# Graph layer on one core: filter banks stored with both channel chunks in a row, taps and stores over two queues each, and two transposes issued earlier in every round

## The chip, the cores and the metric

One core of a Trainium2 chip. The metric is the device time in microseconds (us) of one execution of the whole program; lower is better. "TensorE" is called PE in the profile, the vector engine DVE, the scalar engine ACT, GpSimd POOL and SyncE SP. All results were correct against the reference.

## The reference, cut to what matters

```python
h = relu(layernorm(x))                       # x: (64 graphs, 256 nodes, 256 channels), fp32
xc = transpose(h, (0, 2, 1))
c = relu(bn1(conv1d(xc, conv1_w)))           # 1 x 1
c = bn2(conv1d(c, conv2_w, pad=8))           # 17 taps, 256 -> 256 channels
x_conv = transpose(relu(c + xc), (0, 2, 1))
s = h @ w_se.T + b_se                        # 3 columns
A = exp(-dist(s)) * adj                      # 256 x 256 per graph
x_nmp = A @ relu(h @ w_msg.T + b_msg)
gi = concat(x_conv, x_nmp) @ w_ih.T + b_ih   # gates of a GRU cell
gh = h @ w_hh.T + b_hh
out = x + gru(gi, gh, h)
```

## The kernel before

The 64 graphs are done in eight rounds of four pairs. The 17-tap convolution is done with a transform of length 16, so its weights are needed as **filter banks**, one per frequency bin. They are made once, in the start: a tile of taps is multiplied with a matrix of points, copied from PSUM to a staging tile `fo` by ACT, and stored to DRAM in `filt`. Every round loads the banks from there as `wb`.

```python
KG = P // TAPS                                # 7 channels x 17 taps = 119 partitions
NG = P // KG
REST = P - NG * KG
taps = stage.tile([KG * TAPS, DC * NG + 1, D], FP, name="taps")
# ...
for dc in range(DC):
    for h in range(3):
        load_taps(dc, h * NG // 3, (h + 1) * NG // 3, nc.sync)
# ...
filt = [dram.tile([DC, P, t.shape[1] // KG, D], FP, name=f"filt{n}") for n, t in enumerate(points)]

def filters(m, j):
    # ... two groups of taps of one channel chunk
    p = acc()                                 # 5 PSUM buffers, shared with conv1 and the gates
    for n, g in enumerate(groups):
        mm(p[:size * kinds, n * D:(n + 1) * D], points[m][:size * TAPS, :size * kinds],
           taps[:size * TAPS, g, :], D, start=True, stop=True)
    t = stage.tile([P, 2, D], FP, name="fo", bufs=6)
    nc.scalar.copy(...)
    nc.sync.dma_start(out=filt[m][dc, ...], in_=t[:size * kinds])
```

In what follows the **embedding** is `s`, the **message** `relu(h @ w_msg.T + b_msg)`, the **aggregation** its product with `A`, and the **gates** are the products with `w_ih` and `w_hh`. To **evict** is to copy a result from PSUM to a tile in SBUF. Each pair is normalised by DVE, transposed by PE, evicted with the relu by ACT to `hT`, and goes through `conv1`, also on PE:

```python
def transpose_h(i):
    HT[i] = work.tile([P, DC, W], FP, name="hT", bufs=6)
    for dc in range(DC):
        p = aux()                             # 3 PSUM buffers
        for j in range(G * MC):
            transpose(chunk(p, j // MC, j % MC), X[i][:, j, dc * P:(dc + 1) * P])
        nc.scalar.activation(HT[i][:, dc, :], p, AF.Relu)
    if i + 2 < B // G:
        load_x(i + 2, nc.scalar if i < 2 else nc.sync)

# the middle of a round
gates(i, 1)
aggregate(i + 2)
pace.flush(normed)
transpose_h(nxt + 1)
pace.flush(halved)
conv1(nxt + 1)
# ...
gates(i + 1, 0)
message(i + 3)
embed(i + 3)
pace.flush(normed)
transpose_h(nxt + 2)
conv1(nxt + 2)
```

In these traces ACT and PE take up their work in the order of the program, so where `conv1` follows its transposes at once, PE has nothing to do until ACT has evicted them.

Of the kernel before, what the change touches and what calls it, by code (L numbers as in the profile page):

```python
# [13 lines left out]
FP = mybir.dt.float32  # L14
# [283 lines left out]
def kernel(  # L298
# [26 lines left out]
    nc = tc.nc  # L325
    P = 128
    B, N, D = x.shape
    G = 2
    GB = 8
    PB = GB // G  # L330
    NB = B // GB
    DC = D // P
    MC = N // P
    W = G * N
    TAPS = c2_wT.shape[1]
# [9 lines left out]
    work = ctx.enter_context(tc.tile_pool(name="work", bufs=1))  # L345
    stage_ctx = ExitStack()
    stage = stage_ctx.enter_context(tc.tile_pool(name="stage", bufs=1))
# [55 lines left out]
    def mm(p, w, v, columns, **kw):  # L403
        nc.tensor.matmul(p, w, v, **kw)  # L404
        pace.tensor(columns)
# [75 lines left out]


    KG = P // TAPS
    NG = P // KG
    REST = P - NG * KG
    taps = stage.tile([KG * TAPS, DC * NG + 1, D], FP, name="taps")

    def load_taps(dc, a, b, eng):
        eng.dma_start(out=taps[:, dc * NG + a:dc * NG + b, :],  # L489
                      in_=c2_wT[dc * P + a * KG:dc * P + b * KG].rearrange("(g k) t o -> (k t) g o", k=KG))  # L490

    PASSES = [range(0, 6), range(6, 12), range(12, 16)]
# [1 line left out]
    for n, bins in enumerate(PASSES):  # L494
        f = filter_points(bins, TAPS)
        m = np.zeros((KG, TAPS, KG, f.shape[1]), np.float32)
        for k in range(KG):
            m[k, :, k] = f
        t = stage.tile([KG * TAPS, KG * f.shape[1]], FP, name=f"points{n}")
        nc.scalar.dma_start(out=t, in_=nc.inline_tensor(m.reshape(KG * TAPS, -1), name=f"points{n}").ap())  # L500
        points.append(t)
    for dc in range(DC):
        for h in range(3):
            load_taps(dc, h * NG // 3, (h + 1) * NG // 3, nc.sync)
        nc.sync.dma_start(out=taps[dc * REST * TAPS:(dc + 1) * REST * TAPS, DC * NG, :],  # L505
                          in_=c2_wT[dc * P + NG * KG:(dc + 1) * P].rearrange("k t o -> (k t) o"))

    ld = const.tile([P, W], FP, name="ld")
    rd = const.tile([P, W], FP, name="rd")
# [56 lines left out]



    filt = [dram.tile([DC, P, t.shape[1] // KG, D], FP, name=f"filt{n}") for n, t in enumerate(points)]

    def filters(m, j):

        kinds = filt[m].shape[2]
        groups = range(2 * j, min(2 * j + 2, DC * NG + 1))
        size = REST * DC if groups[0] == DC * NG else KG
        p = acc()
        for n, g in enumerate(groups):
            mm(p[:size * kinds, n * D:(n + 1) * D], points[m][:size * TAPS, :size * kinds],
               taps[:size * TAPS, g, :], D, start=True, stop=True)
        t = stage.tile([P, 2, D], FP, name="fo", bufs=6)  # L580
        nc.scalar.copy(t[:size * kinds, :len(groups)].rearrange("p n o -> p (n o)"),
                       p[:size * kinds, :len(groups) * D])
        if size == KG:
            dc, g = divmod(groups[0], NG)
            nc.sync.dma_start(out=filt[m][dc, g * KG:(g + 2) * KG].rearrange("(g k) t o -> (k t) g o", k=KG),
                              in_=t[:size * kinds])
        else:
            for dc in range(DC):
                nc.sync.dma_start(out=filt[m][dc, NG * KG:].rearrange("k t o -> (k t) o"),
                                  in_=t[dc * REST * kinds:(dc + 1) * REST * kinds, 0, :])  # L590


    WB = {}
# [1 line left out]
    def load_bin(b, n):  # L595
        b, n = b + n // BINS, n % BINS
        if b < NB:
            WB[b, n] = work.tile([P, DC, 3, D], FP, name="wb", bufs=3)
            kinds, m = 3 if n < BINS - 1 else 2, n // len(PASSES[0])
            first = 3 * (n - PASSES[m][0])  # L600
            nc.sync.dma_start(out=WB[b, n][:, :, :kinds, :].rearrange("p k t o -> p k (t o)"),
                              in_=filt[m][:, :, first:first + kinds, :].rearrange("k p t o -> p k (t o)"))


    def operands(n):
# [11 lines left out]

    def products(b, m):
        load_bin(b, 2 * m + 2)
        p = [acc() for _ in range(3)]  # L620
        for n in range(2):
            for kind, v in enumerate(operands(2 * m + n)):
                if v is None:
                    continue
                for o in range(DC):
                    for k in range(DC):
                        mm(p[kind][:, (n * DC + o) * P:(n * DC + o + 1) * P],
                           WB[b, 2 * m + n][:, k, kind, o * P:(o + 1) * P],
                           v[:, k::DC, 0, :], P, start=(k == 0), stop=(k == DC - 1))
        load_bin(b, 2 * m + 3)  # L630
        p1 = work.tile([P, W], FP, name="p1")
        pv = [t.rearrange("p (n a e) -> p a n e", n=2, e=NW) for t in (p1, p[1], p[2])]
        if m < 7:
            nc.scalar.copy(p1, p[0])
            if m < 4:
                re, im = Yv(m % 2, m // 2 * 2, 2), Yv(m % 2, 4 + m // 2 * 2, 2)
            elif m < 6:
                re, im = Yu(m - 4, 0, 2), Yu(m - 4, 2, 2)
            else:
                t = Yu.t[:, :, :, 6:8, :].rearrange("p a c n e -> p n a c e")  # L640
                re, im = t[:, 0], t[:, 1]
            pace.vector(2 * W, pace.pe + PSUM)
            nc.vector.tensor_sub(re, pv[0], pv[2])
            nc.vector.tensor_add(im, pv[0], pv[1])
        else:
            half = W // 2
            nc.scalar.copy(p1[:, :half], p[0][:, :half])
            nc.scalar.mul(Yu(0, 4)[:, :, 0, :], p[0][:, half:].rearrange("p (a e) -> p a e", e=NW), 0.5)
            nc.scalar.mul(Yu(1, 4)[:, :, 0, :], p[1][:, half:].rearrange("p (a e) -> p a e", e=NW), 0.5)
            pace.vector(W, pace.pe + PSUM)  # L650
            nc.vector.tensor_sub(Yu(0, 5)[:, :, 0], pv[0][:, :, 0], pv[2][:, :, 0])
            nc.vector.tensor_add(Yu(1, 5)[:, :, 0], pv[0][:, :, 0], pv[1][:, :, 0])
# [143 lines left out]

    w_ih = const.tile([P, 2 * DC, 3 * D], FP)
    w_hh = const.tile([P, DC, 3 * D], FP)
    chunks = (range(NG // 2), range(NG // 2, NG + 1))
    steps = [(m, j) for m, dc in ((0, 0), (1, 0), (0, 1), (2, 0), (1, 1), (2, 1)) for j in chunks[dc]]  # L800
    transpose_h(0)
    norm(1)
    w_se = const.tile([P, DC, KD], FP)
# [22 lines left out]
    forward()  # L826
    for j, (m, n) in enumerate(steps[PB * 4:]):
        filters(m, n)
        if j == 20:
            load_bin(0, 0)  # L830
            load_bin(0, 1)
    nc.scalar.dma_start(out=w_hh, in_=hh_wT.rearrange("(k p) o -> p k o", p=P))
# [15 lines left out]
    for b in range(NB):  # L848
# [50 lines left out]
        gates(i, 0, wait)  # L899
        transpose_a(i + 2)  # L900
        gates(i, 1)
        aggregate(i + 2)
        pace.flush(normed)
        transpose_h(nxt + 1)
        pace.flush(halved)
        conv1(nxt + 1)
        stats, scale = norm_steps(nxt + 2)
# [2 lines left out]
        pace.add(scale, normed)  # L910
        pace.flush(joined[1])
        gates(i + 1, 0)
        message(i + 3)
        embed(i + 3)
        pace.flush(normed)
        transpose_h(nxt + 2)
        conv1(nxt + 2)
        stats, scale = norm_steps(nxt + 3)
        pace.add(stats)
# [65 lines left out]
```

## Time and profile before

| | before |
|---|---|
| median of three runs | 1997.85 us (1995.75 to 2002.09) |
| PE busy | 1922 us, 96% of the span |
| idle of PE in the start, 0 to 220 us | 47 us |
| waits of PE in the seven steady rounds | 19.4 us, 14 waits, all for `hT` |
| last filter matmul | 111.7 us |

In the profile a group such as `PE L404 MATMUL acc<-hT,w_c` is read as: engine, source line, operation, the tile written and the tiles read; L404 is the line of the helper that issues every matmul. `[2.47 <-ACT hT L537]` at its end means that the engine was idle for 2.47 us before it and that ACT's write of `hT` ended this.

The dearer of the two places of a round is seen in the timeline of PE in the kernel before (start in us, duration in us, what):

```profile
731.73 1.04 PE L408 MATMUL aux<-ident,x 128*128 128x128 f32 x8
735.24 5.32 PE L404 MATMUL acc<-hT,w_c 128*128 128x512 f32 x8 [2.47 <-ACT hT L537]
...
971.67 3.70 PE L404 MATMUL acc<-hT,w_c 128*128 128x512 f32 x8 [2.47 <-ACT hT L537]
```

The last line is the same place one round later. The timeline of ACT shows what the eviction waits behind, the first and the last of the four small activations of `embed`:

```profile
731.93 0.68 ACT L668 ACTIVATE ld<-aux,b_se 3x512 f32<-3x512 f32 x1 [0.30 <-PE aux L404]
...
733.88 0.68 ACT L671 ACTIVATE rd<-aux,b_se 3x512 f32<-3x512 f32 x1
734.59 1.09 ACT L537 ACTIVATE hT<-aux 128x512 f32<-128x512 f32 x2
```

### The profile page before, as it was taken

The page shows a single profiled execution, that of the slowest core. Times are in us where ns is not written, and L with a number is a line of the kernel's source. Part 1 is how long each engine was busy: PE and PEld are TensorE (multiplying, and loading weights), DVE is VectorE, ACT ScalarE, POOL GpSimd, SP SyncE. Part 2 cuts the span into 40 slices and gives each one's busy share as a digit, 9 for nine tenths or more (in the row PEclk, how much of TensorE's full clock was granted, in tenths as well). Part 3 has the DMA queues.
Part 4 walks back from the last instruction along what each step waited for, and adds up shares of the span by engine and source line. Part 5 has one row for each costly group of instructions (what it writes and reads, how often), then busy time and mean ns, then how long its engine had stood idle before and what let it go on. Part 6 is the DMA issues. An engine that isn't in the chain of part 4 may idle for free.

```text
span 1999.7 us, 21268 instructions
## 1 busy us (share of the span) xinstructions
PE 1922.1 (96%) x7966; PEld 1210.7 (61%) x7966; DVE 1401.8 (70%) x2668; ACT 642.2 (32%) x1050; POOL 170.1 (9%) x250
## 2 busy tenths in 40 slices
PE   4879999999999999999999999999999999999997
PEld 2668445875459645695457854486445954568543
DVE  3668738995489945998369963899559993689522
ACT  1533322243222432235222433134322252233321
POOL 3000000010100000010000100001010100000000
PEclk8899999999999999999999999999999999999999
DMA  5785012640217212271115501263032711145010
GB/s 152 222 253 179 22 42 54 176 135 12 78 33 223 73 33 68 78 220 31 41 50 153 161 15 49 62 190 106 23 78 53 233 32 48 32 108 157 11 42 21
DMA packets 91699, 187.12 MB, mean 94 GB/s; under 512 B 20524, under 2 KB 37420, under 8 KB 91596
## 3 DMA queue, kind: packets, MB, share of 16 engines
q1 hardware_dynamic: 60722, 131.87, 21.1%
q0 software_dynamic: 27792, 50.07, 10.9%
q10 hardware_dynamic: 3082, 3.83, 0.7%
q8 instruction: 62, 1.02, 0.2%
q14 instruction: 41, 0.34, 0.0%
HBM read 156.55 MB, written 29.10 MB: 93 GB/s over the span
## 4 chain that ended last, share of the span: by engine, by line
PE 92%; DMA 4%; ACT 2%; SPq 1%; issue 1%; POOL 0%; ACTq 0%; DVE 0%; POOLq 0%; DVEq 0%
PE acc L404 72%; PE aux L404 16%; PE aux L408 3%; DMA wb<-filt 1%; DMA taps<-in_c_wT_dram 1%; DMA filt<-fo 1%; SPq L489 1%; ACT hT L537 0%; SPq L505 0%; DMA bn_m<-in_bn_m_dram 0%; ACT ld L670 0%; ACT rd L671 0%; ACT ld L668 0%; ACT xnm L720 0%; ACT rd L669 0%
## 5 line engine op out<-in xcount | busy, mean ns | idle before, releaser
L404 PE MATMUL acc<-hT,w_hh 128*128 128x512 f32 x768 | 350.6, 592 | 0.0
L404 PE MATMUL acc<-xnm,w_ih 128*128 128x512 f32 x768 | 350.5, 592 | 0.0
L404 PE MATMUL acc<-Yv,w_ih 128*128 128x512 f32 x768 | 340.0, 592 | 0.0
L404 PEld LDWEIGHTS acc<-xnm,w_ih 128*128 128x128 f32 x768 | 145.9, 190 | 183.7 <-issue 183.7
L404 PEld LDWEIGHTS acc<-Yv,w_ih 128*128 128x128 f32 x768 | 145.9, 190 | 183.7 <-issue 181.5
L404 PEld LDWEIGHTS acc<-hT,w_hh 128*128 128x128 f32 x768 | 143.4, 190 | 157.8 <-issue 151.4
L748 ACT ACTIVATE tr<-acc,b_rz 128x512 f32<-128x512 f32 x64 | 44.0, 687 | 557.2 <-PE acc L404 557.2
L750 DVE SCALAR_TENSOR_TENSOR gn<-tr,gn 128x512 f32<-128x512 f32 x64 | 44.2, 690 | 238.0 <-ACT tr L748 238.0
L404 PE MATMUL acc<-hT,w_c 128*128 128x512 f32 x256 | 127.1, 643 | 33.4 <-ACT hT L537 33.4
L404 PE MATMUL acc<-V,wb 128*128 128x128 f32 x1024 | 125.5, 276 | 0.0
L404 PE MATMUL acc<-U,wb 128*128 128x128 f32 x1024 | 122.1, 275 | 0.0
L404 PEld LDWEIGHTS acc<-U,wb 128*128 128x128 f32 x1024 | 120.0, 192 | 1.2
L404 PEld LDWEIGHTS acc<-V,wb 128*128 128x128 f32 x1024 | 120.3, 193 | 0.0
L58 DVE SCALAR_TENSOR_TENSOR V<-T,V 128x256 f32<-128x256 f32 (+2 forms) x224 | 119.8, 606 | 0.3
L404 PE MATMUL aux<-w_msg,hT 128*128 128x256 f32 x512 | 115.8, 379 | 0.0
L404 PE MATMUL aux<-aT,msg 128*128 128x256 f32 x512 | 115.8, 379 | 0.0
L404 PEld LDWEIGHTS aux<-w_msg,hT 128*128 128x128 f32 x512 | 96.1, 190 | 19.6 <-issue 8.1
L404 PEld LDWEIGHTS aux<-aT,msg 128*128 128x128 f32 x512 | 96.1, 190 | 19.2 <-issue 5.7
L775 DVE TENSOR_TENSOR y<-aux,y 128x512 f32<-128x512 f32 x64 | 41.1, 684 | 93.0 <-PE aux L408 93.0
L404 PEld LDWEIGHTS acc<-hT,w_c 128*128 128x128 f32 x256 | 50.7, 207 | 90.2 <-ACT hT L537 44.0
L776 POOL DMA_DIRECT2D out_dram<-y x64 | 39.0, 614 | 729.9 <-DVE y L775 728.6
L372 POOL DMA_DIRECT2D adj<-in_adj_dram x62 | 37.2, 604 | 629.7 <-DVE e L699 605.3
(130 smaller groups left out, 2698.5 us busy)
## 6 DMA issues: line engine op xcount, KB each, us to landing
wb<-filt SPq DMA_DIRECT2D x120, 768.0 KB
y<-in_x_dram POOLq DMA_DIRECT2D x64, 256.0 KB, 5.5
out_dram<-y POOLq DMA_DIRECT2D x64, 256.0 KB, 5.0
adj<-in_adj_dram POOLq DMA_DIRECT2D x62, 256.0 KB, 5.6
x<-in_x_dram SPq DMA_DIRECT2D x60, 256.0 KB
filt<-fo SPq DMA_DIRECT2D x36, 252.0 KB
taps<-in_c_wT_dram SPq DMA_DIRECT2D x6, 714.0 KB
wb<-filt SPq DMA_DIRECT2D x8, 512.0 KB
```

The lines of the kernel that those rows point to most:

```text
L58: return self.step(out, lambda: self.v.scalar_tensor_tensor(out, x, s, y, op0=ALU.mult, op1=ALU.add))
L372: eng.dma_start(out=row_tile(t, g), in_=rows(src, G * i + g))
L404: nc.tensor.matmul(p, w, v, **kw)
L408: nc.tensor.transpose(p, v, ident)
L489: eng.dma_start(out=taps[:, dc * NG + a:dc * NG + b, :], in_=c2_wT[dc * P + a * KG:dc * P + b * KG].rearrange("(g k) t o -> (k t) g o", k=KG))
L748: nc.scalar.activation(tr, pr, AF.Tanh, bias=b_rz[:, dc:dc + 1], scale=0.5)
L750: nc.vector.scalar_tensor_tensor(gn, tr, 1.0, gn, op0=ALU.add, op1=ALU.mult)
L775: nc.vector.tensor_add(row_tile(Y[i], g), p, row_tile(Y[i], g))
L776: nc.gpsimd.dma_start(out=rows(out, G * i + g), in_=row_tile(Y[i], g))
```

## The change

It has two independent parts. **The banks:** the taps get a dimension for the channel chunk, so one filter step makes both chunks of seven channels; a stored row is 2 KB where it was 1 KB, and a bank row 6 KB where it was 3 KB. Half of the taps go over ACT's queue, and the stores of odd groups over GpSimd's. With this the steps run in a new order, and the first two bank loads go out eight steps earlier. The intent is faster transfers in the start. **The moves:** two transposes of each round are issued ahead of the aggregation and ahead of the message and the embedding. The intent is that ACT evicts them while PE has other work.

```diff
-    REST = P - NG * KG
-    taps = stage.tile([KG * TAPS, DC * NG + 1, D], FP, name="taps")
+    NG = -(-P // KG)
+    taps = stage.tile([KG * TAPS, NG, DC, D], FP, name="taps")
 ...
+    for h in range(3):
+        for dc in range(DC):
+            load_taps(dc, h * (NG - 1) // 3, (h + 1) * (NG - 1) // 3, nc.scalar if dc else nc.sync)
 ...
-    filt = [dram.tile([DC, P, t.shape[1] // KG, D], FP, name=f"filt{n}") for n, t in enumerate(points)]
+    filt = [dram.tile([P, t.shape[1] // KG, DC, D], FP, name=f"filt{n}") for n, t in enumerate(points)]
 ...
+        for dc in range(DC):
+            mm(p[:size * kinds, dc * D:(dc + 1) * D], points[m][:size * TAPS, :size * kinds],
+               taps[:size * TAPS, g, dc, :], D, start=True, stop=True)
+        t = stage.tile([P, W], FP, name="fo", bufs=6)
+        nc.scalar.copy(t[:size * kinds], p[:size * kinds])
+        (nc.gpsimd if g % 2 else nc.sync).dma_start(
+            out=filt[m][g * KG:g * KG + size].rearrange("k t c o -> (k t) (c o)"), in_=t[:size * kinds])
 ...
-        if j == 20:
+        if j + PB * 4 == 2 * NG - 10:        # first two bank loads: after step 28 (36 in the kernel before)
             load_bin(0, 0)
             load_bin(0, 1)
 ...
         gates(i, 1)
-        aggregate(i + 2)
         pace.flush(normed)
         transpose_h(nxt + 1)
+        aggregate(i + 2)
         pace.flush(halved)
         conv1(nxt + 1)
 ...
         gates(i + 1, 0)
+        pace.flush(normed)
+        transpose_h(nxt + 2)
         message(i + 3)
         embed(i + 3)
-        pace.flush(normed)
-        transpose_h(nxt + 2)
         conv1(nxt + 2)
```

More of the change, by code (lines that the diff above doesn't have):

```diff
@@ L483 @@
     KG = P // TAPS
-    NG = P // KG
-    REST = P - NG * KG
-    taps = stage.tile([KG * TAPS, DC * NG + 1, D], FP, name="taps")
+    NG = -(-P // KG)
+    taps = stage.tile([KG * TAPS, NG, DC, D], FP, name="taps")
     def load_taps(dc, a, b, eng):
-        eng.dma_start(out=taps[:, dc * NG + a:dc * NG + b, :],
+        eng.dma_start(out=taps[:, a:b, dc, :],
                       in_=c2_wT[dc * P + a * KG:dc * P + b * KG].rearrange("(g k) t o -> (k t) g o", k=KG))
@@ L501 @@
         points.append(t)
+    for h in range(3):
+        for dc in range(DC):
+            load_taps(dc, h * (NG - 1) // 3, (h + 1) * (NG - 1) // 3, nc.scalar if dc else nc.sync)
     for dc in range(DC):
-        for h in range(3):
-            load_taps(dc, h * NG // 3, (h + 1) * NG // 3, nc.sync)
-        nc.sync.dma_start(out=taps[dc * REST * TAPS:(dc + 1) * REST * TAPS, DC * NG, :],
-                          in_=c2_wT[dc * P + NG * KG:(dc + 1) * P].rearrange("k t o -> (k t) o"))
+        last = c2_wT[dc * P + (NG - 1) * KG:(dc + 1) * P]
+        nc.sync.dma_start(out=taps[:last.shape[0] * TAPS, NG - 1, dc, :], in_=last.rearrange("k t o -> (k t) o"))
     ld = const.tile([P, W], FP, name="ld")
@@ L565, in split_steps, with filters @@
         return q
-    filt = [dram.tile([DC, P, t.shape[1] // KG, D], FP, name=f"filt{n}") for n, t in enumerate(points)]
-    def filters(m, j):
-        kinds = filt[m].shape[2]
-        groups = range(2 * j, min(2 * j + 2, DC * NG + 1))
-        size = REST * DC if groups[0] == DC * NG else KG
-        p = acc()
-        for n, g in enumerate(groups):
-            mm(p[:size * kinds, n * D:(n + 1) * D], points[m][:size * TAPS, :size * kinds],
-               taps[:size * TAPS, g, :], D, start=True, stop=True)
-        t = stage.tile([P, 2, D], FP, name="fo", bufs=6)
-        nc.scalar.copy(t[:size * kinds, :len(groups)].rearrange("p n o -> p (n o)"),
-                       p[:size * kinds, :len(groups) * D])
-        if size == KG:
-            dc, g = divmod(groups[0], NG)
-            nc.sync.dma_start(out=filt[m][dc, g * KG:(g + 2) * KG].rearrange("(g k) t o -> (k t) g o", k=KG),
-                              in_=t[:size * kinds])
-        else:
-            for dc in range(DC):
-                nc.sync.dma_start(out=filt[m][dc, NG * KG:].rearrange("k t o -> (k t) o"),
-                                  in_=t[dc * REST * kinds:(dc + 1) * REST * kinds, 0, :])
+    filt = [dram.tile([P, t.shape[1] // KG, DC, D], FP, name=f"filt{n}") for n, t in enumerate(points)]
+    def filters(m, g):
+        kinds = filt[m].shape[1]
+        size = min(KG, P - g * KG)
+        p = acc()
+        for dc in range(DC):
[5 more added lines that the diff above has]
+            out=filt[m][g * KG:g * KG + size].rearrange("k t c o -> (k t) (c o)"), in_=t[:size * kinds])
     WB = {}
@@ L597, in load_bin @@
         if b < NB:
-            WB[b, n] = work.tile([P, DC, 3, D], FP, name="wb", bufs=3)
+            WB[b, n] = work.tile([P, 3, DC, D], FP, name="wb", bufs=3)
             kinds, m = 3 if n < BINS - 1 else 2, n // len(PASSES[0])
             first = 3 * (n - PASSES[m][0])
-            nc.sync.dma_start(out=WB[b, n][:, :, :kinds, :].rearrange("p k t o -> p k (t o)"),
-                              in_=filt[m][:, :, first:first + kinds, :].rearrange("k p t o -> p k (t o)"))
+            nc.sync.dma_start(out=WB[b, n][:, :kinds], in_=filt[m][:, first:first + kinds])
     def operands(n):
@@ L627, in products @@
                         mm(p[kind][:, (n * DC + o) * P:(n * DC + o + 1) * P],
-                           WB[b, 2 * m + n][:, k, kind, o * P:(o + 1) * P],
+                           WB[b, 2 * m + n][:, kind, k, o * P:(o + 1) * P],
                            v[:, k::DC, 0, :], P, start=(k == 0), stop=(k == DC - 1))
@@ L798 @@
     w_hh = const.tile([P, DC, 3 * D], FP)
-    chunks = (range(NG // 2), range(NG // 2, NG + 1))
-    steps = [(m, j) for m, dc in ((0, 0), (1, 0), (0, 1), (2, 0), (1, 1), (2, 1)) for j in chunks[dc]]
+    steps = [(m, g) for m in range(len(PASSES)) for g in range(NG)]
     transpose_h(0)
```

## The prediction

> **What bounds the kernel now.** I read the page first (busy shares, chain), then what TensorE (PE) waits for, then the stretches of time, then the order of instructions at the places where it waits.
>
> From the page of the kernel before, the busy shares and the chain that ended last:
>
> ```profile
> PE 1922.1 (96%) x7966; PEld 1210.7 (61%) x7966; DVE 1401.8 (70%) x2668; ACT 642.2 (32%) x1050; POOL 170.1 (9%) x250
> PE 92%; DMA 4%; ACT 2%; SPq 1%; issue 1%; POOL 0%; ACTq 0%; DVE 0%; POOLq 0%; DVEq 0%
> ```
>
> TensorE is busy for 1922 of 1999.7 us; all there is to win without removing matmuls is 77.6 us. What it waits for, in the whole run and then only between 230 and 1800 us (wait totals: us, times, longest):
>
> ```profile
> PE acc L404 <- ACT hT L537: 33.4, 16, 13.7
> PE aux L408 <- DVE x L436: 10.7, 1, 10.7
> PE acc L404 <- DMA wb<-filt: 10.1, 2, 8.6
> PE acc L404 <- DMA taps<-in_c_wT_dram: 7.1, 2, 6.7
> PE acc L404 <- ACT h L550: 3.4, 1, 3.4
> PE acc L404 <- ACT fo L581: 1.6, 1, 1.6
> ...
> PE acc L404 <- ACT hT L537: 19.4, 14, 2.5
> ```
>
> The busy time by stretch (width, then PE, PEld, DVE, ACT and POOL busy, then clock, DMA share, GB/s):
>
> ```profile
> 0.00:220.00 220.00, 173.00 (x864) 130.43 (x865) 144.76 (x309) 82.31 (x141) 27.89 (x44) 0.92 0.62 186
> 480.00:1800.00 1320.00, 1303.59 (x5352) 809.12 (x5351) 966.09 (x1822) 419.52 (x680) 109.45 (x157) 1.00 0.31 86
> 1800.00:2000.00 200.00, 188.60 (x718) 112.88 (x716) 98.88 (x175) 55.47 (x91) 11.96 (x20) 0.98 0.21 58
> ```
>
> So the idle time splits in three: 220 - 173 = 47 us in the start (input, filter banks, first products), 19.4 us in the seven steady rounds (14 waits, two a round, all for the evicted transposes hT), and 11.4 us in the tail, which no edit touches. The prediction is two sums: the steady 19.4 and what part of the 47.
>
> **What the Trainium skill says.** (1) "DMA: Bandwidth & Descriptors", section "Why a DMA increments its semaphore by 16 and not by 1": a transfer from SP or ACT runs on the largest number of engines up to 16 that divides the slowest dimension. The taps have 119 rows, so 7 engines; the stores 126 rows, so 14. The trace agrees: the DMA share is 0.50 while taps load (7 of 16 is 0.44) and 0.85 in the store stage (14 of 16 is 0.875):
>
> ```profile
> 32.00:44.00 12.00, 8.55 (x32) 5.70 (x30) 2.11 (x4) 2.41 (x4) 0.00 (x0) 0.93 0.50 168
> 80.00:100.00 20.00, 20.00 (x95) 15.87 (x94) 19.93 (x37) 13.12 (x23) 0.00 (x0) 1.00 0.85 267
> 600.00:606.00 6.00, 6.00 (x42) 5.59 (x41) 5.75 (x15) 1.19 (x3) 0.00 (x0) 1.00 0.87 262
> ```
>
> (2) Same page, "Issuing engines are not separate DMA queues": transfers of all issuing engines interleave on the same 16 engines; a second issuer saves only issue time. The trace before has no such pair to compare; I take it as it stands. (3) Same page, "Why small descriptors are slow (HBM only)": about 3 cycles per packet beside one cycle per 32 B; my estimate from it is 3/35 = 9% at 1 KB and 3/67 = 4% at 2 KB. The trace doesn't show even that: 1 KB stores move 267/(16 x 0.85) = 19.6 GB/s per busy engine, the 3 KB bank loads of the third line 262/(16 x 0.87) = 18.8. (4) "TensorE: Matmul & The Clock Gate", Part 1: after an idle window TensorE runs at half clock until it has been busy for some us. The trace agrees: clock 0.50 from 44 to 60 us, and the first conv1 after that wait takes 6.13 us where 3.6 is usual.
>
> **The transposes moved up.** In each round two transposes are followed at once by the conv1 that needs their eviction. The timeline has the dear one at 731.73 us: transposes, then an idle 2.47 us before conv1, because ACT does the embedding's four activations (0.68 each, 731.9 to 734.6) ahead of the hT eviction. The other stands at 706.24, idle 0.30. Sum 2.77 a round, x 7 = 19.4, the total above. After the change, 16 aggregate passes (3.46 us) stand between the first pair, message and embed (3.46 + 1.72 = 5.2 us) between the second, and ACT evicts hT ahead of the message. Eviction takes 1.1 us for both halves: hidden in both places. What must be ready earlier is the normalised x. For the first pair DVE wrote it at 688 us, against 702.8, where the transposes would now stand; for the second at 715.9, against 726.6. Slack 14 and 10 us; the DVE order of these rounds is unchanged in the built program. PSUM for transposes has three buffers, of which the message reuses one that hT freed 1 us before. I see no new wait: **-19 us**.
>
> **The filter banks.** Matmuls: 111 become 114 (the rest groups no longer pair), 3 x 2 x 0.217 us = +1.3 us. Work of TensorE otherwise equal: 57 steps of four passes, 0.868 us each. The start before, from the timeline: taps land piece by piece until 52.0 us; SP issues its first filter store at 45.6, behind all taps; six staging buffers are then full, ACT hangs in the fo copy until 55.9 and the third hT with it, so PE waits 13.7 us and resumes at 57.8. From there it is nearly unbroken until the last filter pass at 111.7. These pieces of the chain carry it (start, us, what):
>
> ```profile
> 32.14 19.88 DMA taps<-in_c_wT_dram
> ...
> 52.08 4.45 DMA filt<-fo
> ...
> 57.77 9.60 PE acc L404 x24
> ```
>
> After: half the taps go over ACT's queue. Both queues feed the same seven engines, so the total rate stays. Against that, the built program shows ACT's loads of the third x waiting (eight semaphores shared by SP and ACT, taken in turn) for the second tap piece of ACT and the third of SP; they stand in ACT's stream ahead of the first conv1 eviction. So ACT should stand still until the third piece has landed, at T. My estimate of T: 52.0 less what no longer goes before it on those engines (x of two graph pairs, w_msg, the adjacency, the remainder piece: 5.8 us at 19 to 22 GB/s an engine) = 46. Until T, TensorE can do one transpose pair, one conv1 and three filter steps (five accumulators). Then, with the durations of the timeline: eviction and copies 4, transposes and conv1 of the second 5, four steps 3.5, third 5, four steps 3.5, fourth 5: the fourth conv1 ends at T + 26 = 72, as before (72.1). 45 steps remain, 39.1 us, so filters end at T + 65 = 111, or 112.5 with a slow clock after the hang; before 111.7. The later start of the steps cancels the earlier landing: **0 +- 6 us**.
>
> Stores over two queues: demand with 126 rows is 252 KB per 0.868 us = 290 GB/s, above the 267 seen on 14 engines, hence 18.9 us of ACT waiting for buffers, of which PE felt 1.6. GpSimd's half may use all 16 engines, so this 1.6 goes, for the 1.3 of added matmuls. The first products then wait 8.6 us for the third bank (issued at 114.8, landed at 130.9, behind late stores, 2.3 MB of gate weights and 1 MB of y). Those stay; a smaller backlog and 6 KB rows may give 2 us. **-2 us**.
>
> In the steady rounds bank loads become 6 KB rows; no PE wait there is for a bank, so nothing.
>
> Sum: -19 - 2 + 0 = -21; 1997.85 - 21 = 1977 us.
>
> **Rivals.** (a) The two queues do help: taps land faster or ACT isn't held, TensorE gets going some 10 us sooner. For it: 7 engines at 168/(16 x 0.50) = 21 GB/s each may have room; against: share already full for those seven. It makes 1962 to 1968. (b) ACT issuing taps holds up hT and the copies beyond T, or x of the third pair arrives late: the start loses 8 to 10 us. For it: three tap issues cost SP 10.4 us, and ACT is strictly in order; against: TensorE has nothing to do then anyway. It makes 1985 to 1988. (c) The earlier transposes wait for DVE or ACT and the 19 us come back: the slack of 10 us speaks against; 1996. (d) The steady gain is hidden anyway: no, those 14 waits lie on the engine of the chain, with nothing else limiting those rounds.
>
> **Range and chances.** The steady part is sure to about 2 us, the start to some 8, run spread is 3 each way: 1965 to 1988. Faster by over 2% means under 1958.7, so another 18 us from the start, of 47 idle: 7%. Slower by over 2% has no mechanism: 1%.
>
> **What would show it.** Right: wait totals between 210 and 1780 us without hT, and each steady round 2.8 us shorter (217.2 instead of 220); DMA share near 0.5 until some 46 us; ACT without work from about 14 (or from its last tap issue) to 46; last filter pass near 112; a bank wait of 6 to 8 us. Wrong: taps in before 40 us or filters done before 105 (rival a); filters after 118 (b); new waits for x or hT in the rounds (c).

## The result, and the profile after

| | before | after |
|---|---|---|
| median of four runs | 1999.97 us (1995.75 to 2002.78) | 1971.97 us (1970.98 to 1973.40) |
| ratio, 95% interval | | 0.9862 (0.9841 to 0.9884) |
| span of the profiled run | 1999.7 us | 1969.0 us |
| mean granted clock of TensorE | 0.986 | 0.992 |

A ratio here and below is the mean time of one kernel's runs over the mean of the other's runs of the same rounds, so it is not quite the ratio of the medians. The gain is 1.4%, 28 us by the medians; the prediction was 21. The two profiled runs differ by 30.6 us, since that of the kernel before took 2001.53 us, 1.6 above its median, and that of the kernel after 1970.98, 1.0 below.

From the page of the kernel after: the busy shares, the chain that ended last, and the group of the `conv1` matmuls (busy us, mean ns of one, idle before them).

```profile
PE 1918.9 (97%) x7972; PEld 1209.2 (61%) x7972; DVE 1402.3 (71%) x2668; ACT 641.9 (33%) x1050; POOL 184.9 (9%) x277
...
PE 92%; DMA 4%; issue 2%; DVE 1%; POOL 0%; ACT 0%; POOLq 0%; ACTq 0%; DVEq 0%
...
L404 PE MATMUL acc<-hT,w_c 128*128 128x512 f32 x256 | 120.5, 615 | 13.6 <-ACT hT L537 13.6
```

PE does six matmul instructions more than before (a matmul of the program is two of them) and yet is busy for 3.2 us less: busy time too has fallen. That is a first sign that some matmuls run faster, not only that gaps are gone.

The wait totals of PE in the kernel after, whole run (us, times, longest):

```profile
PE acc L404 <- ACT hT L537: 13.6, 3, 13.0
PE aux L408 <- DVE x L436: 12.5, 2, 10.9
PE acc L404 <- ACT h L550: 4.1, 1, 4.1
PE acc L404 <- DMA wb<-filt: 3.6, 3, 2.9
PE acc L404 <- ACT fo L580: 3.1, 2, 2.9
...
PE aux L404 <- DVE msg L675: 1.7, 1, 1.7
```

Of the 14 waits for `hT` in the steady rounds none is left; the same view between 230 and 1780 us is empty. The three that remain are in the start. The waits for taps are gone and those for banks are down from 10.1 to 3.6 us, but the wait for staging buffers (`fo`) has doubled from 1.6 to 3.1, and one for the message is new.

The busy time by stretch after (width, then PE, PEld, DVE, ACT and POOL busy, clock, DMA share, GB/s):

```profile
0.00:220.00 220.00, 181.51 (x874) 132.59 (x875) 146.12 (x312) 82.59 (x141) 42.50 (x71) 0.95 0.61 186
480.00:1780.00 1300.00, 1299.90 (x5421) 814.50 (x5420) 976.29 (x1836) 420.79 (x683) 112.04 (x161) 1.00 0.29 90
```

In the steady stretch PE is busy for 1299.90 of 1300 us. The place in the round that was shown above now reads, in PE's timeline of the kernel after:

```profile
715.86 1.04 PE L408 MATMUL aux<-ident,x 128*128 128x128 f32 x8
716.73 3.62 PE L404 MATMUL aux<-w_msg,hT 128*128 128x256 f32 x16
720.18 1.88 PE L404 MATMUL aux<-hT,w_se 128*67 128x512 f32 x4
721.90 3.60 PE L404 MATMUL acc<-hT,w_c 128*128 128x512 f32 x8
```

There is no gap, and `conv1` takes 3.60 us. It does so in every round of the kernel after, where in the seven rounds before it took 5.40, 3.70, 5.32, 3.70, 5.21, 3.70 and 5.16.

**Where the time came from.** I compared the start of the same events in the two traces. The first gate matmul starts at 199.68 us before and at 197.83 after: the whole start is worth 1.85 us. From there the lead grows with each round to 6.84, 10.15, 15.06, 18.35, 23.16, 26.46 and 31.21 us. So the seven rounds are worth 31.21 - 1.85 = **29.4 us**, in steps of 5.0, 3.3, 4.9, 3.3, 4.8, 3.3 and 4.8. The small steps are the rounds in which `conv1` took 3.70 us before, the large ones those in which it took over 5. The sum can be built: 19.4 us of recorded waits; 14 x 0.27 = 3.8, because transposes with a gap behind them take their full 1.04 us instead of a pitch of 0.87 (716.73 - 715.86), and a `conv1` that starts from empty 3.70 instead of 3.60 (called **refill** below); and the four slow `conv1`, 5.40 + 5.32 + 5.21 + 5.16 - 4 x 3.70 = 6.3. Together 29.5.

That the slow ones are a matter of the clock is seen when the kernel before is read by stretches that hold just those matmuls, the slow one and that of the next round:

```profile
735.24:740.39 5.15, 5.15 (x8) 2.21 (x9) 0.00 (x0) 1.21 (x2) 0.00 (x0) 0.68 0.22 85
...
971.67:975.21 3.54, 3.54 (x9) 1.58 (x10) 0.00 (x0) 1.22 (x2) 0.00 (x0) 1.00 0.36 135
```

The granted clock is 0.68 in the first and 1.00 in the second, and 5.15 x 0.68 = 3.5 us: the same work at a lower clock.

**The start.** The timeline of PE in the kernel after, the groups with the longest waits and those around the filters:

```profile
26.15 6.01 PE L404 MATMUL acc<-hT,w_c 128*128 128x512 f32 x8 [12.98 <-ACT hT L537]
...
38.84 2.07 PE L404 MATMUL acc<-taps,points 119*126 119x256 f32 x4 [4.08 <-ACT h L550]
...
52.20 1.74 PE L408 MATMUL aux<-ident,x 128*128 128x128 f32 x8 [1.59 <-DVE x L436]
54.18 5.40 PE L404 MATMUL acc<-hT,w_c 128*128 128x512 f32 x8 [0.25 <-ACT hT L537]
...
94.73 1.09 PE L404 MATMUL acc<-taps,points 119*77 119x256 f32 x4 [2.88 <-ACT fo L580]
96.02 16.52 PE L404 MATMUL acc<-taps,points 119*77 119x256 f32 x68 [0.20 <-ACT fo L580]
112.46 1.93 PE L404 MATMUL aux<-hT,w_se 128*67 128x512 f32 x4
...
126.06 1.73 PE L404 MATMUL acc<-Sv,wb 128*128 128x128 f32 x8 [2.85 <-DMA wb<-filt]
...
136.36 1.83 PE L404 MATMUL aux<-rd,ld 67*128 67x256 f32 x4 [1.68 <-DVE msg L675]
```

And what ACT does in that time:

```profile
9.39 14.79 ACTq L488 DMA_DIRECT2D taps<-in_c_wT_dram  x3
...
34.09 3.78 ACTq L372 DMA_DIRECT2D x<-in_x_dram  x2
38.00 1.45 ACT L550 ACTIVATE h<-acc,bn_shift,bn_scale 128x512 f32<-128x512 f32 x2 [11.41 <-DMA taps<-in_c_wT_dram]
```

ACT issues its three taps pieces until 24.2 us, evicts the first `hT` until 26.6 us, and then does no work for 11.4 us: its two loads of x wait for pieces of taps (they are issued at 34.1 and 37.3 us), and only behind them does it evict the first `conv1`. The filters end at 112.46 us, before at 111.71. The 13.7 us wait for the third `hT` that the kernel before had has gone and a wait of 13.0 us for the first has come. What the start gains is the wait for the third bank: 8.56 us before, 2.85 after. Against this stand a longer wait for staging buffers and the new wait for the message.

### The profile page after: what moved, and what is told of

Read it like the earlier page. It is cut to its first block, busy times and chain, and to the rows that moved or that the text cites. A ratio compares the mean times of both kernels' runs of the same rounds, so it can differ in the third digit from the quotient of the medians.

```text
span 1969.0 us, 21300 instructions
## 1 busy us (share of the span) xinstructions
PE 1918.9 (97%) x7972; PEld 1209.2 (61%) x7972; DVE 1402.3 (71%) x2668; ACT 641.9 (33%) x1050; POOL 184.9 (9%) x277
## 4 chain that ended last, share of the span: by engine, by line
PE 92%; DMA 4%; issue 2%; DVE 1%; POOL 0%; ACT 0%; POOLq 0%; ACTq 0%; DVEq 0%
PE acc L404 72%; PE aux L404 17%; PE aux L408 4%; DMA taps<-in_c_wT_dram 1%; DMA w_ih<-in_ih_wT_dram 1%; DMA filt<-fo 1%; DMA x<-in_x_dram 0%; DMA wb<-filt 0%; POOL filt L581 0%; DMA w_c<-in_c_wT_dram 0%; ACT fo L580 0%; POOL rstd L433 0%; POOL out_dram L767 0%; DVE x L436 0%; DVE st L427 0%
## 5 line engine op out<-in xcount | busy, mean ns | idle before, releaser
L404 PE MATMUL acc<-hT,w_c 128*128 128x512 f32 x256 | 120.5, 615 | 13.6 <-ACT hT L537 13.6
L372 POOL DMA_DIRECT2D adj<-in_adj_dram x62 | 37.3, 606 | 620.2 <-DVE e L690 606.6
```

The costliest lines, as they stand in the source:

```text
L372: eng.dma_start(out=row_tile(t, g), in_=rows(src, G * i + g))
L404: nc.tensor.matmul(p, w, v, **kw)
```

## The experiments

Twelve kernels were run. All outputs are right. Those of one batch shared a chip and the runs of the kernel before: 2000.2 us (median of 11) for the first batch, 2000.24 (of 12) for the second, 2001.46 (of 6) for the third. The first batch holds the four runs named e, the second f1, f2, f3 and g1, the third f5 and the three named h.

### The two parts alone

**e1_moves_only** is the kernel before with both moves and nothing else.

```diff
         gates(i, 1)
-        aggregate(i + 2)
         pace.flush(normed)
         transpose_h(nxt + 1)
+        aggregate(i + 2)
 ...
         gates(i + 1, 0)
-        message(i + 3)
-        embed(i + 3)
         pace.flush(normed)
         transpose_h(nxt + 2)
+        message(i + 3)
+        embed(i + 3)
         conv1(nxt + 2)
```

> The kernel before with the two transposes moved up and nothing else. Theory A (my prediction's term: only the recorded idle time is lost at a wait): -19.4 us, ratio 0.990. Theory B (each wait also costs a refill of the pipeline of about 0.27 us, and where the clock falls to half after a 2.47 us gap, conv1 takes 5.4 in place of 3.6 us): -29 us, ratio 0.9853, spread of runs narrower; the wait totals of the steady rounds hold no hT. Both: the first 200 us as before to within 1 us.

Measured: 1973.01 us (1971.82 to 1974.95), ratio 0.9864 (0.9850 to 0.9877). That is 27 us, so the reading that each stall costs refill and clock beside its idle time holds, and the sum of idle times alone, 19.4, falls. From the first gate matmul to the same event of the last steady round the trace is 28.2 us shorter. The expected start, as before to within 1 us, was missed: the first gate matmul is at 198.15 us, against 199.68 in the kernel before, with nothing changed ahead of it. In e3 and e4 below, whose starts are unchanged too, it is at 196.14 and 199.44. So two traces of one start can differ by 3.5 us there; the end of the filters differs by 1.6 us among these four.

**e2_banks_only** is the kernel after with the two moves undone.

```diff
         gates(i, 1)
+        aggregate(i + 2)
         pace.flush(normed)
         transpose_h(nxt + 1)
-        aggregate(i + 2)
 ...
         gates(i + 1, 0)
-        pace.flush(normed)
-        transpose_h(nxt + 2)
         message(i + 3)
         embed(i + 3)
+        pace.flush(normed)
+        transpose_h(nxt + 2)
         conv1(nxt + 2)
```

> The changed kernel with the two transposes put back, so the filter banks, stores and taps alone. Theory A (the start gives what the two sums left: 27.6 - 19.4): -8 us, ratio 0.996. Theory B (the start gives only the 1.9 us by which the first gate matmul stands earlier in the changed kernel's trace): -2 us, ratio 0.999, with the steady rounds at their old length.

Measured: 2000.10 us (1998.86 to 2002.46), ratio 0.9998 (0.9986 to 1.0010). The banks with their queues are worth nothing that five rounds can see. The 14 waits for `hT` are all there, 19.4 us again. In this profile three of the seven `conv1` behind the 2.47 us gap are slow (5.24, 5.17 and 5.40 us), not four.

Which rounds are slow can be read from the clock records of the two traces. All changes of the granted clock in a trace lie on a grid of 3.413 us, and a fall in a steady round lasts one step of it (735.12 to 738.53 us in the kernel before). In the seven slow places, four there and three in e2, the clock falls between 0.43 us before the start of `conv1` and 0.22 after it, so that nearly the whole step before the fall lies on the transposes and the gap, together 3.51 us. In the other seven the last grid point before `conv1` lies 0.48 to 1.18 us ahead of it, with more of other matmuls in the step, and the clock stays. So the place of the gap on the grid tells the slow places from the others in all fourteen; no run was made to shift it. A slow and a fast round of the kernel before together last some 471 us, or 138 steps, which is why every other round is slow there.

### Why the moves gave more than the idle time

**e3_second_move** moves only the second transpose, the one with the 2.47 us gap.

```diff
         gates(i + 1, 0)
-        message(i + 3)
-        embed(i + 3)
         pace.flush(normed)
         transpose_h(nxt + 2)
+        message(i + 3)
+        embed(i + 3)
         conv1(nxt + 2)
```

> The kernel before with only the second of the two moves (transposes ahead of message and embedding). Theory A (idle only): 7 x 2.47 = -17.3 us, ratio 0.9914. Theory B (idle, refill, half clock): 7 x (2.47 + 0.27) + 4 x 1.65 = -25.8 us, ratio 0.987; the first kind of wait stays, 0.30 us in each of 7 rounds, and costs 0.57 each.

Measured: 1973.88 us (1972.12 to 1976.96), ratio 0.9869 (0.9854 to 0.9883). The gain of 26 us comes from waits that sum to 7 x 2.47 = 17.3. The wait totals of PE in the steady rounds show what is left, the first place of each round:

```profile
PE acc L404 <- ACT hT L537: 2.1, 7, 0.3
```

Every `conv1` behind the second place takes 3.60 us. So nearly the whole gain belongs to one place. By the medians the other is worth 0.9 us, with intervals that overlap, but e3's start happened to be 2.0 us earlier than e1's. Over the seven rounds of the traces the gain is 25.4 us in e3, 28.2 in e1 and 29.4 in the kernel after, so the other place is worth 2.8 to 4.0 us; 7 x 0.57 = 4.0 was expected.

**e4_filler** leaves both places as they were and puts three matmuls that nobody reads into the 2.47 us gap. PE has more work, and the gap isn't closed for `conv1`, which starts as late as before; only the idle time is filled.

```diff
         transpose_h(nxt + 2)
+        if nxt + 2 < B // G:
+            filler = acc()
+            for c in (W, W, D):
+                nc.tensor.matmul(filler[:, :c], w_hh[:, 0, :P], HT[i + 3][:, 0, :c], start=True, stop=True)
         conv1(nxt + 2)
```

> The kernel before, with three matmuls nobody reads (2.15 us of TensorE work) put between the second transposes and their conv1 in each round, where TensorE idles 2.47 us. Right results. Theory A (a wait costs its idle time, the clock is of no account): no change, 0 +- 1 us, ratio 1.000. Theory B (the gap drops the clock in about every other round): conv1 after it takes 3.6 to 3.7 us in every round, -6 us, ratio 0.997, though there is more work.

Measured: 1994.63 us (1991.61 to 1996.23), ratio 0.9967 (0.9954 to 0.9980). The same place as above, in PE's timeline of this kernel:

```profile
729.81 1.04 PE L408 MATMUL aux<-ident,x 128*128 128x128 f32 x8
730.68 2.31 PE L920 MATMUL acc<-hT,w_hh 128*128 128x512 f32 x6
733.31 3.70 PE L404 MATMUL acc<-hT,w_c 128*128 128x512 f32 x8 [0.32 <-ACT hT L537]
```

From the transposes to `conv1` it is 3.50 us, in the kernel before 3.51. But `conv1` takes 3.70 us in all seven rounds. The steady part of this trace is 6.3 us shorter than that of the kernel before, exactly the surplus of the four slow `conv1`. The kernel with useless work added is the faster one. This isolates the clock: what the gap cost beyond its length was that the clock sometimes fell after it.

### Where the gain of the two queues went

These start from the kernel after and undo or add one thing in the start. The ends of the filters and the first gate matmul are more telling than the whole time, since the rounds that follow are the same.

**f1_taps_sp**: all taps over SP's queue, stores still over two.

```diff
-            load_taps(dc, h * (NG - 1) // 3, (h + 1) * (NG - 1) // 3, nc.scalar if dc else nc.sync)
+            load_taps(dc, h * (NG - 1) // 3, (h + 1) * (NG - 1) // 3, nc.sync)
```

> The changed kernel with all taps issued by SP, in the same order of pieces. In the changed kernel the last tap piece landed at about 43.5 us (before: 52.0), and ACT stood still until 37.9. Theory A (two queues feeding the same seven engines move more than one): the last piece lands 6 us or more later, 49 to 52 us, with 130 to 150 GB/s in place of 170 to 180 between 12 and 32 us. Theory B (my prediction's: the engines set the rate, the rest is what else was in line): it lands at 43 to 45 us with the same GB/s. ACT is free early in both; time of the whole within 5 us of the changed kernel.

Measured: 1968.66 us (1967.37 to 1971.10), ratio 0.9844 (0.9829 to 0.9860). The taps do land later, SP's first store starts at 49.2 us instead of 43.5. The second queue thus moves the same bytes faster. And yet the filters end earlier, at 108.66 us, and the first gate matmul is at 194.45, 3.4 us before that of the kernel after. ACT doesn't have to issue taps and is free for its evictions: the first `conv1` starts at 12.8 us, in the kernel after at 26.15. (3.4 us is within what two traces of one start can differ by, 3.5 us; the 3.8 us at the end of the filters are beyond their 1.6.)

**f2_stores_sp**: taps over two queues, all stores over SP.

```diff
-        (nc.gpsimd if g % 2 else nc.sync).dma_start(
+        nc.sync.dma_start(
```

> The changed kernel with all filter stores issued by SP. In the changed kernel ACT waits for staging buffers from 82 to 95 us and TensorE loses 2.9 us at 91.9 plus a slow clock. Theory A (stores from GpSimd land late): the wait shrinks to under 1 us and the last filter pass ends 3 to 5 us earlier than 112.5. Theory B (the two bank loads of 1.5 MB issued at 83.4 take the engines from the stores, whoever issues them): the wait of 2 to 5 us stays, near 85 to 97 us. Whole: within 5 us of the changed kernel.

Measured: 1965.25 us (1964.00 to 1966.56), ratio 0.9824 (0.9811 to 0.9837). PE's timeline of this kernel:

```profile
49.99 1.74 PE L408 MATMUL aux<-ident,x 128*128 128x128 f32 x8 [0.25 <-DVE x L436]
51.98 3.70 PE L404 MATMUL acc<-hT,w_c 128*128 128x512 f32 x8 [0.25 <-ACT hT L537]
...
90.93 15.01 PE L404 MATMUL acc<-taps,points 119*77 119x256 f32 x68 [2.12 <-ACT fo L580]
```

The stall for staging buffers is here too, 2.12 us against 2.88 + 0.20, so it isn't made by the queue of GpSimd. The gain is in part elsewhere. In the kernel after the third pair's normalised x comes late (52.20 us, a wait of 1.59 for DVE) and its `conv1` runs for 5.40 us, here 3.70. What is late is x itself: DVE can start on the second half of it at 49.34 us, here at 47.14. The small operation that GpSimd does in each normalisation holds DVE for 1.15 us in both, so it isn't held up by the stores. The other traces agree (49.0 and 49.2 us in e2 and g1, with stores over GpSimd; 47.4 in f5, without). That the early stores of GpSimd, from 40.7 us, take the transfer engines from x fits this, but isn't shown. The filters end at 105.87 and the first gate matmul is at 191.22, 6.6 us earlier than after.

**h3_paired_one_queue**: both undone, everything over SP, as in the kernel before but with the paired rows.

> The changed kernel with all taps and all stores on SP: what is left of the filter-bank change is the pairing (2 KB rows, 6 KB bank rows) and the new order of steps. Theory A (each second queue costs: 3.4 us for the taps by the one-queue-taps run, 6.6 us for the stores by the one-queue-stores run, and the two add up): the first gate matmul stands at 187 to 190 us in place of 197.8, -8 to -10 us against the changed kernel's 1972. Theory B (they overlap, since both remove the same late start): 190 to 192, as with the stores alone.

Measured: 1974.33 us (1973.11 to 1975.63), ratio 0.9857 (0.9839 to 0.9874). Both readings fell: nothing carried over from f1 and f2. The old hold came back, as ACT's timeline shows:

```profile
56.77 1.29 ACT L580 COPY fo<-acc 126x512 f32<-126x512 f32 x2 [9.42 <-DMA filt<-fo]
57.95 1.09 ACT L537 ACTIVATE hT<-aux 128x512 f32<-128x512 f32 x2
```

SP's first store waits behind all the taps until 51 us, the six staging buffers are full, and ACT hangs in its copy with the next `hT` behind it, as in the kernel before. The wait for taps is 8.5 us, where the kernel before has 7.1 in two. Four runs make a square; since the medians are of three batches, the columns of the trace are the ones to compare. Each is a single trace, with the spread named under e1 (1.6 us at the end of the filters, 3.5 at the first gate matmul):

| taps over | stores over | kernel | filters end | first gate matmul | median us |
|---|---|---|---|---|---|
| SP | SP | h3_paired_one_queue | 117.7 | 203.2 | 1974.33 |
| SP | SP and GpSimd | f1_taps_sp | 108.7 | 194.5 | 1968.66 |
| SP and ACT | SP | f2_stores_sp | 105.9 | 191.2 | 1965.25 |
| SP and ACT | SP and GpSimd | after | 112.5 | 197.8 | 1971.97 |

Either second queue alone frees the hold, and is worth 9 to 12 us to the first gate matmul. Both together cost 3 to 7 us against either alone. The effects don't add because they remove the same wait, while each has a cost of its own: the taps keep ACT from its evictions, and with GpSimd's stores x comes later.

**g1_early_fold**: the kernel after, with a few tiny operations on the second batch norm (`fold_bn(bn2)` and two sums of biases) moved ahead of the filters.

```diff
     b_ih, b_hh = vec(ih_b, "b_ih"), vec(hh_b, "b_hh")
+    s2, h2_shift = fold_bn(bn2, "bn2", 1.0 / L)
+    b_rz = ...                               # the lines for b_rz and b_se2, unchanged
     for j in range(PB):
 ...
     pace.flush(odd)
-    s2, h2_shift = fold_bn(bn2, "bn2", 1.0 / L)
-    b_rz = ...
```

> The changed kernel with the second batch norm's scale and shift and two bias sums computed before the filters, so that VectorE needn't wait for GpSimd, which is behind the last stores and the y loads (VectorE idle from 95.8 to 116.5 us). Theory A (after the shorter bank wait it is VectorE's even transform that holds the first products, 117 to 137 us): the TensorE wait for the message (1.7 us) goes, VectorE does the even transform from 96 us, and the first gate matmul stands 3 to 6 us earlier than 197.8. Theory B (the bank loads hold that stretch, VectorE is hidden behind them): the wait moves to the banks and the gate matmul moves by under 1.5 us.

Measured: 1966.58 us (1964.97 to 1969.13), ratio 0.9831 (0.9816 to 0.9847). What it removes is seen in DVE's timeline of the kernel after:

```profile
95.66 0.16 DVE L469 TENSOR_SCALAR bn_scale<-bn_v 128x2 f32<-128x2 f32 x1
116.54 0.16 DVE L471 TENSOR_TENSOR bn_scale<-bn_scale,bn_g 128x2 f32<-128x2 f32 x1 [20.71 <-POOL bn_scale L470]
```

DVE waits 20.7 us for one operation on a 128 x 2 tile, because it stands in GpSimd's stream behind the stores and the loads of y. DVE's next transform is late by that, and the message behind it. In g1 that transform starts at 95.56 us, the wait for the message is gone, and the first gate matmul is at 193.88, 4.0 us earlier than after.

**f5_late_banks**: f2 with the first two bank loads issued after the last filter step, to see whether they cause the stall for staging buffers.

```diff
-        if j + PB * 4 == 2 * NG - 10:
+        if j + PB * 4 == 3 * NG - 1:
             load_bin(0, 0)
```

> The run with all stores on SP, with the loads of the first two banks moved from the middle of the filters to behind the last one. Theory A (the 5.4 us in which ACT waits for staging buffers near 85 to 90 us come from these 1.5 MB on the same engines): that wait is under 1 us, the filters end near 103.5 in place of 105.8, and TensorE then waits 6 us or more for the first bank, so the gate matmul stands later than 191.2. Theory B (stores of 290 GB/s on 14 engines are too many by themselves): the wait of TensorE for the copies stays at 1.5 us or more.

Measured: 1968.23 us (1967.98 to 1968.83), ratio 0.9829 (0.9813 to 0.9844). PE's timeline of this kernel:

```profile
64.19 39.71 PE L404 MATMUL acc<-taps,points 119*126 119x256 f32 x180
103.83 1.93 PE L404 MATMUL aux<-hT,w_se 128*67 128x512 f32 x4
117.56 2.04 PE L404 MATMUL acc<-Sv,wb 128*128 128x128 f32 x8 [11.79 <-DMA wb<-filt]
```

The filters now run unbroken, so the stall came from the bank loads; that they take the transfer engines from the stores is the likely way, but isn't shown. Moving them only trades it for a wait of 11.8 us at the first bank; the first gate matmul is at 195.2 us, 4 us later than in f2. (The times are of different batches; the ratios, 0.9829 and 0.9824, can't tell the two apart.) The stall buys banks that come in time.

### The rate of the taps

**f3_taps16**: the kernel after, with each load of taps cut in rows 0 to 112 and 112 to 119. By the rule that the prediction quotes, 119 rows give 7 engines and 112 rows 16.

```diff
+        src = c2_wT[dc * P + a * KG:dc * P + b * KG].rearrange("(g k) t o -> (k t) g o", k=KG)
+        for r in (slice(0, 112), slice(112, KG * TAPS)):
+            eng.dma_start(out=taps[r, a:b, dc, :], in_=src[r])
-        eng.dma_start(out=taps[:, a:b, dc, :], in_=...)
```

> The changed kernel with each tap load cut into rows 0 to 111 (16 divides 112) and rows 112 to 118. Theory A (119 rows keep a load on seven engines, and these set the pace): the DMA share in 12 to 28 us rises from 0.5 to 0.8 or more, the taps land by about 30 us in place of 43.5, and the last filter pass ends some 8 us earlier, so -4 to -8 us for the whole. Theory B (another limit, such as HBM rows of 1 KB or the queue): share and landing as in the changed kernel.

Measured: 1963.73 us (1961.70 to 1964.03), ratio 0.9814 (0.9801 to 0.9827). One stretch of the kernel after while taps load, then the same stretch of f3 (the last two columns are the DMA share of 16 engines, which packets in flight at once can take above 1, and GB/s):

```profile
16.00:24.00 8.00, 0.00 (x0) 0.00 (x0) 1.42 (x4) 0.00 (x0) 7.15 (x12) 1.00 0.55 175
```

```profile
16.00:24.00 8.00, 0.71 (x1) 0.50 (x2) 1.87 (x5) 2.37 (x3) 6.82 (x11) 1.00 1.11 246
```

The share doubles and the rate rises by 40%. The filters end at 105.6 us, the first gate matmul is at 190.44, 7.4 us earlier. The cut is worth that on top of both second queues.

### A version from what was learned

**h1_best** puts together the taps cut in 112 + 7 rows, the early fold, and everything over SP. **h2_best_two_tap_queues** is the same with the taps over SP and ACT:

```diff
-            load_taps(dc, h * (NG - 1) // 3, (h + 1) * (NG - 1) // 3, nc.sync)
+            load_taps(dc, h * (NG - 1) // 3, (h + 1) * (NG - 1) // 3, nc.scalar if dc else nc.sync)
```

> All that helped together, taps and stores on SP: taps cut to 112 and 7 rows, stores on SP, the second batch norm folded early. If the gains (3.4, 6.6, 7.4 and 4.0 us) overlapped not at all: -21 us against the changed kernel, 1951. I expect them to overlap, since TensorE alone needs 113 us to the first products and 76 from there: the first gate matmul at 180 to 186, the whole 1955 to 1960, ratio 0.977 to 0.980.

> As the run before, but with the taps on the queues of SP and ACT as in the changed kernel. Theory A (with all 16 engines busy a second queue brings nothing, and ACT is held by issuing taps and by the x loads that wait for them): ACT's first eviction at 21 us or later in place of 13, and 2 to 4 us slower than the run before. Theory B (a second queue still moves more): taps land 2 us or more earlier and the whole is as fast or faster.

Measured: h1 1958.40 us (1957.55 to 1959.46), ratio 0.9779 (0.9764 to 0.9795); h2 1956.70 us (1955.87 to 1958.48), ratio 0.9772 (0.9756 to 0.9787). The same stretch of h1, then of h2:

```profile
16.00:24.00 8.00, 6.18 (x26) 4.18 (x24) 2.70 (x9) 3.45 (x6) 7.53 (x12) 1.00 0.95 201
```

```profile
16.00:24.00 8.00, 0.31 (x1) 0.31 (x2) 2.19 (x5) 2.24 (x3) 7.17 (x11) 1.00 1.12 255
```

I had two readings for h2, slower by 2 to 4 us because ACT issues, or as fast or faster because the taps come sooner. The first falls. h1 lies in its expected range of 1955 to 1960 us. The first gate matmul is at 186.03 us in h1 and at 183.04 in h2; the difference in time is small and the intervals overlap. Against the kernel before, h2 gains 16.6 us in the start and the rest in the rounds. It beats both kernels.

## Why the prediction was right or wrong

**The total.** 1977 us was predicted, 1971.97 measured, inside the range. The difference is one term, the steady one, and it was the surest in my eyes.

**The steady term, "-19 us".** The mechanism was right in all its parts: the two places, ACT's order, the slack of x, no new wait, as the empty wait list and e1 show. The size was not: 29.4 us instead of 19.4. The step that failed is the one that set the cost of a stall equal to its recorded idle time. e3, e4 and the clock of the two stretches show what was missing: 3.8 us of refill in 14 places, and 6.3 us of `conv1` at a lower clock. The evidence was in view. The prediction quotes the half clock after a wait in its fourth place from the skill and uses it for the start only, and the `conv1` of 5.32 us stands in the very lines it read for the 2.47 us gap. The sign to look for ("each steady round 2.8 us shorter (217.2 instead of 220)") was therefore off too: the rounds are 3.3 and 4.8 to 5.0 us shorter in turn. The 220 is no round but the width of the stretches; a round, all but the last, took 234.8 or some 236.4 us before and takes 231.5 after.

**The start, "0 +- 6 us" and "-2 us".** In sum right: 1.85 us in the trace, nothing in the times of e2, and four traces of one unchanged start differ by up to 3.5, so 1.85 can't be told from nothing. Its parts were less right.

- The hold of ACT was predicted and is there, and the filters end at 112.46 us where 112.5 was predicted. But T was 46 in the prediction; ACT was released at 38.0 us, after the piece of SP, and the last piece of ACT landed at about 43.5, which I take from SP's first store starting then. The step "both queues feed the same seven engines, so the total rate stays" is what failed: between 16 and 32 us f1 moves 153 GB/s on one queue, the kernel after 174 on two. The difference holds beyond this pair: the six traces with 119-row taps on one queue show 138 to 155 there, the five on two queues 162 to 174.
- What this won was lost again, in x late by GpSimd's stores (f2), in slow clocks after the gaps and in the stall for buffers. That the end came out right to 0.1 us is a cancellation, not a proof of the sum.
- "GpSimd's half may use all 16 engines, so this 1.6 goes" is wrong: the wait grew to 3.1 (how many engines the stores of GpSimd use, no view here shows). f5 shows that it belongs to the two bank loads. (The 290 GB/s of this sum should be 297: 252 KB were taken as 252,000 bytes. Nothing hangs on it.)
- The wait for the third bank was to fall by 2 us and fell by more than 5. No wait for a bank is longer than 1.8 us in h3, which has neither second queue, so this belongs to the rows, the new order or the earlier bank loads; these were not separated. The new wait of 1.7 us for the message was not foreseen; g1 shows that its cause is GpSimd's stream.

**The rivals.** (a) held in its first half, taps did land sooner, but was worth nothing in the end, as the square of four shows. (b) held for ACT, which did stand still, and x of the third pair did come late, but only with GpSimd's stores (1.6 us): in f2, with ACT held in the same way, the wait is 0.25. The loss of 8 to 10 us didn't come. (c) and (d) fell: no new waits, and the 14 waits paid in full and more.

**What stays open.** Why two queues move more over the same engines than one; h1 and h2 agree that they do, but whether it is the queue or the issuing engine being held back was not separated. How GpSimd's stores make x late. And whether the transposes ahead of the 2.47 us gap count as idle time for the clock, since every gap that was followed by a slow clock in the steady rounds has them.

## What to carry to other kernels

A gap on the bounding engine can cost more than its length, here 29.4 us for 19.4 us of recorded idle time: look at the duration of the instructions just behind it, in every round and not in one, and count the refill and the slower clock. Before adding a second queue, ask which wait it removes and what the engine that issues for it has to do promptly; two such changes can remove the same wait and then only their costs add. The number of rows of a transfer matters: cut from 119 rows into 112 and 7, the taps raised the DMA share from 0.55 to 1.11, which won 7 us here on top of both.

## What the Trainium skill lacked or had wrong

- "DMA: Bandwidth & Descriptors", section "Issuing engines are not separate DMA queues", says that issuing from several engines only saves the time of issuing. Here a second queue also raised the rate with the same rows: 153 GB/s (f1) against 174 (after) with 119 rows, from 16 to 32 us, and 204 (h1) against 247 (h2) with 112 and 7 rows, from 8 to 24 us. Whether it was the queue or issuing that had been too slow was not settled; in the latter case the page stands.
- "TensorE: Matmul & The Clock Gate", Part 1, gives the idle window after which the clock falls as about 3.4 us and says that the window runs freely. The traces agree with both (the grid of 3.413 us under e2). What they add is that a recorded gap of 2.47 us can be enough: with the transposes ahead of it 3.51 us, it brought the clock down in four rounds of seven before and in three in e2. The gaps of 0.3 us in the same rounds never did. Whether the transposes count as idle time was not tested, so this is no contradiction.
